# A four-layer graph network on one core: layer 1's small feature maps stand at two places per step, and its first two products run in halves by turns

## The chip, the core and the metric

The kernel runs on one core of a Trainium2 chip. The metric is device time in microseconds of one launch; the median of several runs is given. In the profile PE is the matrix engine (TensorE), PEld its weight loads, DVE the vector engine, ACT the scalar engine, POOL GpSimd, and SP the engine whose queue issues most of the DMAs.

## The reference, cut to what matters

Eight graphs `x` of 2048 nodes with 64 features share one adjacency matrix. Four layers follow one another, each of them residual behind a layer norm and a ReLU. The change is in layer 1, which repeats one update three times, and touches layer 2:

```python
# adj: 2048 x 2048, symmetric pattern, every row divided by its number of ones
h = maximum(layernorm(x), 0)                       # layer 1
v = h;  v[:, 0] = intervention_value
for _ in range(3):
    effects = einsum('nm,bmd->bnd', adj, v)
    t = relu(einsum('bnk,dk->bnd', concatenate([v, effects], -1), W1) + b1)
    v = einsum('bnk,dk->bnd', t, W2) + b2
x = x + v
h = maximum(layernorm(x), 0)                       # layer 2
agg = einsum('ij,bjf->bif', adj, h)
...
x = x + (einsum('bnf,of->bno', agg_nl, w_out) + b_out)
```

Layer 0 is a Chebyshev graph convolution with node-wise weights, and layer 3 an attention that comes down to the mean over the nodes for this input.

## The kernel before

**Tiling.** Graphs are worked on in pairs (`p` = 0 to 3), so that 2 x 64 features fill 128 partitions. The 2048 nodes are 16 chunks of 128 (index `m`) and 4 blocks of 512 (index `nb`). `BT` holds the pattern of the adjacency matrix as ones and zeros for the whole kernel; the division by the row's count is done on the result, with a row `crow` that is loaded anew for each block.

**A product.** `product(hl, nb, ...)` multiplies an operand by block `nb` of `BT`: for each of the 16 chunks two matmuls of 128x128 by 128x512 (L257), one with the high part `H` of the operand and one with the low rest `L`, 32 in all, into one PSUM bank of the tag "mm" (two banks). `fill` maps a chunk number to a function that is called behind that chunk, so that other work is written between the matmuls. `scaled` (L247, DVE) then multiplies the sum by `crow`. The operand `hl` is a list of four pairs (H, L), one for each block of 512 nodes; chunk `m` reads pair `m // 4`. `halves` makes a pair: a cast on ACT (L237) and a subtraction on DVE (L239).

**Layer 1.** The kernel folds W2 into the matrices of the next step, so that each of the three steps (`s`) of a pair has four products and two kinds of small maps, both made of 64x64 tiles because the two graphs of a pair are kept apart:

- `map_two(nb)` (L939, "ph" in the profile): the map of the previous features of blocks `nb` and `nb + 1`, four programmed matmuls of 512 columns, into two banks of the tag "big"; four copies on ACT (L945) put the result back in place. Before the change it is called at chunk 10 of blocks 0 and 2.
- `back_to_nodes` (L692, "bn"): the map of one block of new features back into node order, 16 programmed matmuls of 64 columns. `finish(nb)` calls it, and then for steps 0 and 1 adds a row (L924, DVE) and makes the pair of halves for the next step; in the last step it adds the map to `acc` (L920), which is x loaded from DRAM, and calls `keep`, which starts the next layer's norm, adds the bias on POOL (L731) and stores x (L732). `finish` of blocks 0 and 1 is called behind the products of blocks 1 and 2, that of block 2 at chunk 8 of block 3 (in the last step behind block 3), that of block 3 at the end of the step.

Between product and map stand the scaling, an addition of the mapped old features (L955, DVE) and the ReLU (L956, ACT). In steps 0 and 1 each block is also followed by two calls of `test`, a comparison on DVE (L885) of a part of the adjacency matrix with its transpose; three buffers of `st` and `mt` are loaded ahead on SP's queue.

In the last step of a pair `prepare_next` makes the operand of the next item block by block: it loads `h` from DRAM, and for layer 1 it writes the intervention row into block 0 (L720, ACT, behind the latest ReLU), transposes the block (L269), and maps it with another `back_to_nodes` ("bn_u") into halves.

**Order of the work.** The layer norm is a generator with three stages; `go_on` advances all pending ones by a stage. A planner sets the order on each engine when the kernel is built: it follows the program's order, but takes a later instruction where it expects an earlier one not to be ready, and `issue_after` pins an instruction behind another one of its engine. Tiles of one tag share a fixed number of buffers, and a tile that takes a buffer waits for the release of its last user. The last `finish(3)` of layer 1 is put off (`put_off`) and called at chunk 9 of the second block of layer 2.

Of the kernel before, what the change touches and what calls it, by code (L numbers as in the profile page):

```python
# [42 lines left out]
def uniform_path(  # L43
# [31 lines left out]
    P = 128  # L75
# [25 lines left out]
    def bank(tag, name):  # L101
        return psums[-1].tile([P, 512], F32, tag=tag, name=name)
# [69 lines left out]

    pending = []
    powers, firsts, variances, scales = [], [], [], []
    squares, lows, stored = [], [], []
    ahead = []
# [35 lines left out]
    def go_on():  # L214

        with tc.issue_after(ahead.pop().ins) if ahead else nullcontext():
            for e in list(pending):
                next(e[0])
                e[1] -= 1
                if e[1] == 0:  # L220
                    pending.remove(e)
        ahead.clear()

    def all_done():
        while pending:
# [18 lines left out]
    def scaled(ps, out, crow):  # L244

        crow, to = (a.rearrange("p (t q) -> p t q", t=4) for a in (crow, out))
        ahead.append(nc.vector.tensor_tensor(  # L247
            to, ps.rearrange("p (q t) -> p t q", t=4), crow, op=ALU.mult
        ))
        return out  # L250

    def product(hl, nb, name, out, crow, fill={}, tag="mm"):

        ps = bank(tag, f"bv_{name}")
        for m in range(NCH):
            for i in range(2):
                nc.tensor.matmul(  # L257
                    ps, hl[m // 4][i][:, m % 4, :], BT[:, m, nb * 512:(nb + 1) * 512],
                    start=(m == 0 and i == 0), stop=(m == NCH - 1 and i == 1),
                )  # L260
            if m in fill:
                fill[m]()
        return scaled(ps, out, crow)

    def transposed(src, name):

# [5 lines left out]
    def to_feat(h, out, name):  # L272
        pt = transposed(lambda t: h[:, t, :], name)
        nc.scalar.copy(out, pt.rearrange("p t n -> p (t n)"))
        return out
# [403 lines left out]

    two = (slice(0, C), slice(C, P))  # L680

    def back_to_nodes(fT, wmat, name):

        ps = psums[-1].tile([P, 2, 512], F32, tag="big", name=f"bn_{name}")
        for t in range(4):
            for hf in range(2):
                for bb in range(2):  # L690
                    at = t * P + hf * C
                    nc.tensor.matmul(  # L692
                        ps[two[hf], bb, t * C:(t + 1) * C],
                        fT[two[bb], at:at + C], wmat[two[bb], two[bb]], start=True, stop=True,
                    )
        return ps[:, :, :4 * C].rearrange("p b (t c) -> p t b c", c=C)

    def back_whole(fT, wmat, name):

# [7 lines left out]
    ops = {}  # L707
    relus = []

    def prepare_next(n, q):  # L710
        if n >= len(items):
            return
        layer, p = items[n]
        nm = f"{layer}_{p}_{q}"
        hl, gT = ops.setdefault(n, ([], []))
        h = load_h(p, q, nm, lastp[0] if n else l0q)
        if layer == 1:
            if q == 0:
                with tc.issue_after(relus[-1].ins) if relus else nullcontext():
                    nc.scalar.copy(h[0:1, 0, :], ivt)  # L720
            gT.append(to_feat(h, feat(0, f"gT_{nm}"), nm))
            h = (back_to_nodes if n else back_whole)(gT[q], w1e, f"u_{nm}")
        hl.append(halves(h, nm))

    def rows4(r):
        return r.rearrange("p (b c) -> p b c", b=2)[:, None].to_broadcast([P, 4, 2, C])

    def keep(p, nb, acc, name, more):

# [44 lines left out]
    for p in range(NP):  # L774
# [21 lines left out]
        def between(nb, t):  # L796

            if 4 * p + nb + 1 == 4 * NP:
                prepare_next(0, t)
            elif nb == 2 and t == 1:  # L800
                halve_next(0)
            elif nb == 3:
                halve_next(t + 1)
                if t == 0:
                    load_next(3)
# [94 lines left out]
        nc.tensor.matmul(pf[:1, :1], tot, ones[:, :1], start=True, stop=True)  # L900
        nc.vector.tensor_scalar(flag, pf[:1, :1], 0.0, None, op0=ALU.is_gt)

    put_off = []

    def layer1(n, p):
        hl, gT = ops[n]
        steps = 3  # L910
        for s in range(steps):
            last = s == steps - 1
            g_new, hl_new = [], []

            def finish(nb):
                nm = f"1_{p}_{s}_{nb}"
                if last:
                    acc = load_x(1, p, nb)
                    pn = back_to_nodes(g_new[nb], w2T, nm)
                    nc.vector.tensor_tensor(nodes(acc), pn, nodes(acc), op=ALU.add)  # L920
                    keep(p, nb, acc, f"2_{p}_{nb}", rows4(rbo))
                else:
                    pn = back_to_nodes(g_new[nb], w1e2, nm)
                    nc.vector.tensor_tensor(pn, pn, rows4(r1e), op=ALU.add)  # L924
                    hl_new.append(halves(pn, nm))

            def mid():
                if last:
                    prepare_next(n + 1, 2)
                else:  # L930
                    finish(2)

            def map_two(nb):

                ph = psums[-1].tile([P, 2, 512], F32, tag="big", name=f"ph_1_{p}_{s}_{nb}")
                w = w1v2 if s else w1vT
                for i in range(2):
                    for bb in range(2):
                        nc.tensor.matmul(  # L939
                            ph[two[bb ^ i], bb, :], w[two[bb], two[bb]], gT[nb + i][two[bb], :],  # L940
                            start=True, stop=True,
                        )
                for i in range(2):
                    for bb in range(2):
                        nc.scalar.copy(gT[nb + i][two[bb], :], ph[two[bb ^ i], bb, :])  # L945

            for nb in range(NB):
                nm = f"1_{p}_{s}_{nb}"
                crow = load_crow(nb, nm)
                g = feat((s + 1) % 2, f"g_{nm}")  # L950
                fill = {8: mid} if nb == 3 else {}
                if nb % 2 == 0:
                    fill[10] = lambda: map_two(nb)
                product(hl, nb, nm, g, crow, fill=fill)
                gadd = nc.vector.tensor_tensor(g, g, gT[nb], op=ALU.add)  # L955
                relus.append(nc.scalar.activation(g, g, AF.Relu, bias=b1s if s else b1c))  # L956
                g_new.append(g)
                go_on()
                if nb in (1, 2):
                    finish(nb - 1)  # L960
                    if last:
                        prepare_next(n + 1, nb - 1)
                if s < 2:
                    k = 2 * (8 * p + 4 * s + nb)
                    with tc.issue_after(gadd.ins):
                        test(k)
                        test(k + 1)
            if last:
                finish(2)
                prepare_next(n + 1, 3)  # L970
            if last and n == NP - 1:

                put_off.append(lambda: finish(3))
            else:
                finish(3)
            gT, hl = g_new, hl_new

# [9 lines left out]
    def finish2(g):  # L989
        p, nb = divmod(g, NB)  # L990
        nm = f"acc_2_{p}_{nb}"
        acc = term(1, nm) if p % 2 else feat(1, nm)
        acc = acc.rearrange("p (j f) -> p j f", j=4)
        accs.append(acc)
        fill_x(acc, 2, p, nb)
        pn = back_to_nodes(es[g], wos, f"2_{p}_{nb}")
        nc.vector.tensor_tensor(nodes(acc), pn, nodes(acc), op=ALU.add)
        norm_relu(acc, f"3_{p}_{nb}", lambda h: zs.update({g: h}))

# [47 lines left out]
    def layer2(n, p):  # L1047
        hl, _ = ops[n]

        def behind(g):  # L1050
            go_on()
            if g > 0:
                finish2(g - 1)
            if g % NB > 1:
                prepare_next(n + 1, g % NB - 2)

        for nb in range(NB):
            g = NB * p + nb
            nm = f"2_{p}_{nb}"
            crow = load_crow(nb, nm)  # L1060
            fill = {5: lambda: behind(g)}
            if g > 0:
                fill[12] = go_on
            if nb == 3:
                fill[8] = lambda: prepare_next(n + 1, 2)
            if g == 1:
                fill[9] = lambda: put_off.pop()()
            if g > 1:
                fill[15] = lambda: sums(g - 2)
            e = lastp[0].tile([P, 512], F32, tag="st", name=f"e_{nm}", bufs=3)  # L1070
            es.append(product(hl, nb, nm, e, crow, fill=fill))
            if g == 0:
                go_on()
        prepare_next(n + 1, 3)
        if p == NP - 1:
            go_on()
            finish2(g)
            sums(g - 1)
            all_done()
            sums(g)  # L1080
# [600 lines left out]
```

## Time and profile before

| what | value |
|---|---|
| runs | 1218.68, 1221.76, 1225.72 us (median 1221.76) |
| the profiled execution, its own time | 1220.42 us |
| its span, first to last instruction | 1218.7 us |
| mean granted clock of TensorE | 0.996 |
| layer 1, first to last big matmul | about 625.7 to 1059.6 us of the span |
| big matmuls "bv<-BT" of layers 1 and 2 (L257, H and L) | 2048, starts 0.2267 us apart when undisturbed |
| node maps with `g` (L692) | 1536 instructions, mean 224 ns |
| feature maps (L939, from `g` and `gT`) | 192 instructions, mean 615 ns |

In the profile one programmed fp32 matmul shows as two instructions, so one `back_to_nodes` is 32 of them and one `map_two` 8. Durations of matmuls overlap, since they are pipelined; distances between starts say what one costs. A row of the chain of waits has the start, the time that the piece took on the chain, the engine, the tile, the line and the number of instructions. A row of the timeline has start, duration, engine, line, operation, the tile written and those read, and the shape.

### The profile page before, as it was taken

How to read it: one execution, taken by the hardware profiler on the slowest of the kernel's cores; microseconds unless marked ns; L12 is line 12 of the kernel's file. 1: busy time of each engine (PE TensorE's matmuls, PEld its weight loads, DVE VectorE, ACT ScalarE, POOL GpSimd, SP SyncE). 2: the span in 40 equal slices, each digit the busy share in tenths (PEclk: the TensorE clock that was granted, in tenths of full speed). 3: DMA queues.
4: the chain of work that ended last, by engine and by line, in shares of the span. 5: the costliest groups of instructions: out<-in, count | busy, mean ns of one | idle time of the engine just before them, and what ended most of it. 6: DMA issues, size and time to landing. Idle time of an engine off the chain costs nothing.

```text
span 1218.7 us, 19540 instructions
## 1 busy us (share of the span) xinstructions
PE 1196.7 (98%) x7730; PEld 812.6 (67%) x7730; DVE 745.2 (61%) x1944; ACT 237.8 (20%) x377; POOL 229.4 (19%) x244
## 2 busy tenths in 40 slices
PE   9999999999999999999999999999999999999996
PEld 7765555555675557655567777777777777777774
DVE  5457888777757775477755535535543645576664
ACT  6610001000010000000022233223323323211100
POOL 5610222211121111011110013003100400241211
PEclk9999999999999999999999999999999999999998
DMA  9981333333332233122237526543653553443321
GB/s 357 356 200 51 93 109 113 82 82 84 91 104 65 65 91 87 54 66 65 61 79 177 126 87 161 128 98 113 163 128 82 150 143 95 128 153 118 118 67 45
DMA packets 99848, 141.24 MB, mean 116 GB/s; under 512 B 43772, under 2 KB 56572, under 8 KB 97700
## 3 DMA queue, kind: packets, MB, share of 16 engines
q1 hardware_dynamic: 81188, 79.16, 24.5%
q0 software_dynamic: 12256, 49.73, 13.9%
q10 hardware_dynamic: 6304, 11.01, 2.9%
q8 instruction: 63, 1.03, 0.3%
q14 instruction: 37, 0.30, 0.1%
HBM read 95.03 MB, written 35.66 MB: 107 GB/s over the span
## 4 chain that ended last, share of the span: by engine, by line
PE 89%; DVE 4%; DMA 3%; issue 1%; POOL 1%; ACT 1%; POOLq 0%; ACTq 0%; DVEq 0%; SPq 0%
PE bv L257 39%; PE y L750 26%; PE bn L692 3%; PE bv_1b L257 2%; PE bv_2b L257 2%; PE bv_3b L257 2%; PE ph L939 2%; PE bv_0b L257 2%; DMA x<-in_x_dram 1%; PE bv_0a L257 1%; PE bv_3a L257 1%; PE pt L269 1%; PE bv_2a L257 1%; PE bv_1a L257 1%; DVE acc L759 1%
## 5 line engine op out<-in xcount | busy, mean ns | idle before, releaser
L257 PE MATMUL bv<-BT,H 128*128 128x512 f32 x1024 | 411.1, 401 | 0.0
L257 PE MATMUL bv<-BT,L 128*128 128x512 f32 x1024 | 401.3, 392 | 0.0
L257 PEld LDWEIGHTS bv<-BT,H 128*128 128x128 f32 x1024 | 192.2, 188 | 62.9 <-issue 22.0
L257 PEld LDWEIGHTS bv<-BT,L 128*128 128x128 f32 x1024 | 192.4, 188 | 37.5
L759 DVE SCALAR_TENSOR_TENSOR acc<-y,emb,acc 128x128 f32<-128x128 f32 x512 | 176.1, 344 | 65.8 <-PE y L750 65.8
L759 DVE SCALAR_TENSOR_TENSOR odd<-y,emb,odd 128x128 f32<-128x128 f32 x448 | 153.2, 342 | 0.0
L750 PE MATMUL y<-wt,t0T 64*128 64x512 f32 x512 | 143.7, 607 | 2.4 <-DVE odd L759 1.7
L200 POOL TENSOR_TENSOR rstd<-var,mhalf 128x8 f32<-128x8 f32 x64 | 105.7, 1654 | 185.9 <-DVE var L197 184.5
L247 DVE TENSOR_TENSOR g<-bv,crow 128x512 f32<-128x512 f32 x48 | 33.2, 691 | 168.5 <-PE bv L257 168.5
L192 ACT ACTIVATE sq<-z 128x512 f32<-128x512 f32 x64 | 40.4, 632 | 396.8 <-DVE z L187 366.5
L750 PEld LDWEIGHTS y<-wt,t0T 64*128 64x128 f32 x512 | 45.8, 185 | 63.3 <-issue 57.1
L731 POOL TENSOR_TENSOR acc<-acc,b2r 128x512 f32<-128x512 f32 x16 | 22.2, 1389 | 317.2 <-DVE z L187 317.2
L731 POOL TENSOR_TENSOR acc<-acc,wl 128x512 f32<-128x512 f32 x16 | 20.5, 1279 | 288.0 <-DVE z L187 288.0
L750 PE MATMUL y<-wt,t1T 64*128 64x512 f32 x256 | 66.8, 589 | 0.0
L203 DVE SCALAR_TENSOR_TENSOR z<-z,rstd 128x512 f32<-128x512 f32 x64 | 44.7, 703 | 28.3 <-POOL rstd L200 28.2
L195 DVE TENSOR_REDUCE var<-sq 128x8 f32<-128x512 f32 x64 | 43.5, 680 | 13.4 <-ACT sq L192 13.4
L885 DVE SCALAR_TENSOR_TENSOR junk<-mt,cols,st 128x512 uint8<-128x512 bf16 x64 | 47.7, 745 | 3.4 <-DMA mt<-MD 3.0
L945 ACT COPY g<-ph 64x512 f32<-64x512 f32 x64 | 37.2, 581 | 48.5 <-PE ph L939 47.7
L750 PEld LDWEIGHTS y<-wt,t1T 64*128 64x128 f32 x256 | 27.1, 187 | 27.8 <-issue 27.8
L956 ACT ACTIVATE g<-g,b1s 128x512 f32<-128x512 f32 x32 | 23.1, 723 | 99.1 <-DVE g L955 98.9
L730 POOL DMA_DIRECT2D hs<-z x32 | 18.7, 585 | 125.8 <-DVE z L203 89.3
L187 DVE TENSOR_TENSOR z<-acc,mean 128x512 f32<-128x512 f32 x56 | 38.3, 691 | 6.1 <-DMA hs<-z 4.7
(225 smaller groups left out, 1657.0 us busy)
## 6 DMA issues: line engine op xcount, KB each, us to landing
BT<-in_adj_dram POOLq DMA_DIRECT2D x16, 1024.0 KB, 10.0
crow<-crowD SPq DMA_DIRECT2D x64, 256.0 KB, 3.4
st<-in_adj_dram SPq DMA_DIRECT2D x64, 256.0 KB, 3.9
hs<-z POOLq DMA_DIRECT2D x40, 256.0 KB, 3.1
xs<-acc POOLq DMA_DIRECT2D x32, 256.0 KB, 2.4
MD<-BT POOLq DMA_DIRECT2D x16, 512.0 KB, 5.6
acc<-xs SPq DMA_DIRECT2D x32, 256.0 KB, 3.4
hb<-hs SPq DMA_DIRECT2D x28, 256.0 KB, 3.6
```

What stands on the lines that cost most here:

```text
L187: firsts.append(nc.vector.tensor_tensor(split(z), nodes(xt), each(mean)[:, :, :, None].to_broadcast([P, 4, 2, C]), op=ALU.subtract))
L192: squares.append(nc.scalar.activation(sq, z, AF.Square))
L195: nc.vector.tensor_reduce(var, groups(sq), axis=AX.X, op=ALU.add)
L200: powers.append(nc.gpsimd.tensor_tensor(rstd, var, mhalf, op=ALU.pow))
L203: scales.append(nc.vector.scalar_tensor_tensor(groups(h), g, 0.0, rstd[:, :, None].to_broadcast([P, 8, C]), op0=ALU.max, op1=ALU.mult))
L257: nc.tensor.matmul(ps, hl[m // 4][i][:, m % 4, :], BT[:, m, nb * 512:(nb + 1) * 512], start=(m == 0 and i == 0), stop=(m == NCH - 1 and i ...
L692: nc.tensor.matmul(ps[two[hf], bb, t * C:(t + 1) * C], fT[two[bb], at:at + C], wmat[two[bb], two[bb]], start=True, stop=True,)
L731: nc.gpsimd.tensor_tensor(nodes(acc), nodes(acc), more, op=ALU.add)
L750: nc.tensor.matmul(y[:, bb, :], terms[k][hs_, ts], wt[hs_, k, dg * 512:(dg + 1) * 512], start=(k == 0), stop=(k == K - 1),)
L759: last = nc.vector.scalar_tensor_tensor(xj, yd, ec, old, op0=ALU.mult, op1=ALU.add)
L885: nc.vector.scalar_tensor_tensor(junk, mt, cols[:, i, :], st, op0=ALU.mult, op1=ALU.not_equal, accum_out=bad[:, i, q:q + 1],)
L945: nc.scalar.copy(gT[nb + i][two[bb], :], ph[two[bb ^ i], bb, :])
```

## The change

The arithmetic stays the same. The order in layer 1 and the shapes of two helpers change:

- `back_two` replaces `back_to_nodes` and maps one or two blocks into one PSUM tile of two banks; for two blocks the row is added in one DVE instruction of 1024 columns, and the halves are made for each block.
- `product` is split into `chunks` (some of the chunks) and the scaling. In each step the order is: first half of block 0; the maps of blocks 2 and 3 carried over from the step before (`carry`); `map_two(0)`; first half of block 1; second half of block 0; second half of block 1; block 2; `map_two(2)` and the maps of blocks 0 and 1; block 3. The maps of blocks 2 and 3 are then carried into the next step.
- `map_two` writes two single banks of the tag "tr" instead of one tile of the tag "big".
- In the last step the second block's `keep` is put into a list `later`, from which `go_on` takes one.
- `prepare_next` becomes `begin_next` (load, intervention row, transposes; for layer 2 the halves) and `halve_two` (the maps of two blocks and their halves). At a change of pair, blocks 0 and 1 of the next pair are begun at chunk 4 of block 3 and mapped at chunk 9, block 2 is begun at chunk 12, block 3 at chunk 4 of the next step's first half, and blocks 2 and 3 are mapped behind the carried maps.
- The carried maps of the very last step, now two blocks, are called at chunk 9 of the second block of layer 2.

```diff
@@ go_on @@
         ahead.clear()
+        if later:
+            later.pop(0)()
@@ product @@
         ps = bank(tag, f"bv_{name}")
-        for m in range(NCH):
+        chunks(ps, hl, nb, range(NCH), fill)
+        return scaled(ps, out, crow)
+
+    def chunks(ps, hl, nb, ms, fill={}):
+        for m in ms:
             for i in range(2):
                 nc.tensor.matmul(
...
@@ back_to_nodes @@
-    def back_to_nodes(fT, wmat, name):
+    def back_two(fTs, wmat, name):
         ps = psums[-1].tile([P, 2, 512], F32, tag="big", name=f"bn_{name}")
...
+        for i, fT in enumerate(fTs):
+            for t in range(4):
+                for hf in range(2):
+                    for bb in range(2):
+                        at = t * P + hf * C
+                        nc.tensor.matmul(
+                            ps[two[hf], bb, (4 * i + t) * C:(4 * i + t + 1) * C],
+                            fT[two[bb], at:at + C], wmat[two[bb], two[bb]],
+                            start=True, stop=True,
+                        )
+        return ps.rearrange("p b (t c) -> p t b c", c=C)
@@ prepare_next @@
-    def prepare_next(n, q):
+    def begin_next(n, q):
...
+        if layer == 2:
+            hl.append(halves(h, nm))
+            return
+        if q == 0:
+            with tc.issue_after(relus[-1].ins) if relus else nullcontext():
+                nc.scalar.copy(h[0:1, 0, :], ivt)
+        gT.append(to_feat(h, feat(0, f"gT_{nm}"), nm))
...
+    def halve_two(n, q):
+        if n < NP:
+            hl, gT = ops[n]
+            ps = back_two(gT[q:q + 2], w1e, f"u_{n}_{q}")
+            for i in range(2):
+                hl.append(halves(ps[:, 4 * i:4 * i + 4], f"u_{n}_{q + i}"))
@@ layer1 @@
+    carry = []
+
+    def step1(n, p, st, hl, gT):
...
+        def map_two(nb):
+            ph = [bank("tr", f"ph_{nm}_{nb}_{bb}") for bb in range(2)]
...
+        def finish_two(nb):
+            ps = back_two(g_new[nb:nb + 2], w2T if last else w1e2, f"{nm}_{nb}")
+            if not last:
+                nc.vector.tensor_tensor(ps, ps, rows4(r1e, 8), op=ALU.add)
+            for i in range(2):
+                pn = ps[:, 4 * i:4 * i + 4]
+                if last:
+                    acc = load_x(1, p, nb + i)
+                    nc.vector.tensor_tensor(nodes(acc), pn, nodes(acc), op=ALU.add)
+                    keep_it = lambda i=i, acc=acc: keep(
+                        p, nb + i, acc, f"2_{p}_{nb + i}", rows4(rbo)
+                    )
+                    later.append(keep_it) if i else keep_it()
+                else:
+                    hl_new.append(halves(pn, f"{nm}_{nb + i}"))
...
+        def add(nb):
+            g = g_new[nb]
+            gadd = nc.vector.tensor_tensor(g, g, gT[nb], op=ALU.add)
+            relus.append(nc.scalar.activation(g, g, AF.Relu, bias=b1s if st else b1c))
+            if not last:
+                k = 2 * (8 * p + 4 * st + nb)
+                with tc.issue_after(gadd.ins):
+                    test(k)
+                    test(k + 1)
+
+        halves_of = range(NCH // 2), range(NCH // 2, NCH)
+        ps0 = sums_of(0)
+        other = n > 0 and st == 0
+        chunks(ps0, hl, 0, halves_of[0], {4: lambda: begin_next(n, 3)} if other else {})
+        if carry:
+            carry.pop()()
+        if other:
+            halve_two(n, 2)
+        map_two(0)
+        ps1 = sums_of(1)
+        chunks(ps1, hl, 1, halves_of[0])
+        chunks(ps0, hl, 0, halves_of[1])
+        scale(ps0, 0)
+        add(0)
+        go_on()
+        chunks(ps1, hl, 1, halves_of[1])
+        scale(ps1, 1)
+        add(1)
+        go_on()
+        ps2 = sums_of(2)
+        chunks(ps2, hl, 2, range(NCH))
+        scale(ps2, 2)
+        map_two(2)
+        finish_two(0)
+        add(2)
+        go_on()
+        fill = {}
+        if last:
+            fill = {
+                4: lambda: (begin_next(n + 1, 0), begin_next(n + 1, 1)),
+                9: lambda: halve_two(n + 1, 0), 12: lambda: begin_next(n + 1, 2),
+            }
+        ps3 = sums_of(3)
+        chunks(ps3, hl, 3, range(NCH), fill)
+        scale(ps3, 3)
+        add(3)
+        go_on()
+        carry.append(lambda: finish_two(2))
+        return hl_new, g_new
...
@@ layer2 @@
             if g == 1:
-                fill[9] = lambda: put_off.pop()()
+                fill[9] = lambda: carry.pop()()
```

`sums_of(nb)` loads `crow` and takes an "mm" bank; `scale` is `scaled` into a new feature tile. `first_operand`, called in layer 0, begins and maps the first pair block by block as before.

## Prediction

> **What bounds the kernel now.** I read the page first: span, busy row, clock row.
>
> ```profile
> PE 1196.7 (98%) x7730; PEld 812.6 (67%) x7730; DVE 745.2 (61%) x1944; ACT 237.8 (20%) x377; POOL 229.4 (19%) x244
> ...
> PEclk9999999999999999999999999999999999999998
> ```
>
> TensorE is busy in every slice at full clock, so time is gained only by shortening its stream. The chain of waits, in order of time, shows what that stream is in layer 1. This is one whole step (pair 0, step 1), from a first big matmul after `map_two(0)` to the next such point:
>
> ```profile
> 666.86 9.76 PE bv L257 x42
> 676.62 0.62 PE bn L692 x32
> 677.25 5.21 PE bv L257 x22
> 682.46 1.02 PE ph L939 x8
> 683.48 2.51 PE bv L257 x10
> 685.99 0.62 PE bn L692 x32
> 686.62 4.30 PE bv L257 x18
> 690.92 0.62 PE bn L692 x32
> 691.55 5.89 PE bv L257 x25
> 697.44 0.62 PE bn L692 x32
> 698.07 2.72 PE bv L257 x11
> 700.79 1.02 PE ph L939 x8
> ```
>
> The 128 big matmuls (bv) of a step are cut at six places by 64x64 work: four node maps (bn, `back_to_nodes`) and two feature maps (ph, `map_two`). The chain never leaves TensorE here: the step, 34.95 us, is a sum of its instructions. The stage table agrees: in this window PE is busy all 34.95 us, DVE 16.41, ACT 9.66, POOL 0. What one place costs is seen in TensorE's timeline:
>
> ```profile
> 641.29 0.39 PE L257 MATMUL bv<-BT,L 128*128 128x512 f32 x1
> 641.60 0.69 PE L692 MATMUL bn<-wl,g 64*64 64x64 f32 x32
> 642.23 0.50 PE L257 MATMUL bv<-BT,H 128*128 128x512 f32 x1
> 642.57 0.39 PE L257 MATMUL bv<-BT,L 128*128 128x512 f32 x1
> 642.80 0.40 PE L257 MATMUL bv<-BT,H 128*128 128x512 f32 x1
> ```
>
> Starts (first column) are what to read, since durations overlap. Undisturbed, bv starts every 0.2267 us. Here the map starts 0.31 after the last bv (0.085 late), takes 0.63, and the second bv after it comes 0.34 after the first (0.11 late), the next ones 0.01 late. Over the whole step: 34.95 - 128 x 0.2267 (29.02) - 4 x 0.625 - 2 x 1.02 = 1.39, or **0.23 us per place** beyond the map itself. Last, two maps that happen to stand side by side (first transition between pairs):
>
> ```profile
> 736.77 0.69 PE L692 MATMUL bn_u<-w1e,gT 64*64 64x64 f32 x32 [0.15 <-ACT gT L274]
> 737.29 0.65 PE L692 MATMUL bn<-wl,g 64*64 64x64 f32 x32
> 737.87 0.50 PE L257 MATMUL bv<-BT,H 128*128 128x512 f32 x1
> ```
>
> Together 1.10 us, not 2 x 0.625 = 1.25: a lone map also contains about 0.15 us in which nothing overlaps its last instructions. The other two transitions show 1.09 for the same pair. (The bracket is a wait ahead of the pair and not in the 1.10.)
>
> **The change, part by part.** The arithmetic and the instructions of TensorE stay; the map order changes. A regular step has two places instead of six: A, after half of block 0 (carried maps of blocks 2 and 3 of the step before, then `map_two(0)`), and B, after block 2 (`map_two(2)`, then maps of blocks 0 and 1). Layer 1 has 12 steps. Before: 12 x 6 = 72 groups, 72 places. After: 12 A, 12 B, and one in layer 2: 25. So 47 joins: 24 of bn to bn (12 at B, 11 at A, one in layer 2), 23 of bn to ph (12 at B, 11 at A, since the first A has no carry).
>
> *bn to bn:* 0.23 + 0.15 = 0.38 by the rows above, x 24 = 9.1 us. A rule of the Trainium skill speaks against this ("TensorE: Matmul & The Clock Gate", section "Wait — 56ns, not 53.3ns?"): start to start never drops under about 25 ns however small the matmul. The row has 32 instructions in 0.52 us, 16 ns each. By the rule a pair would need 1.6 us, joining would save only the 0.23, and this term would be 5.5 us. The row is of this very instruction, so I take 9.1.
>
> *bn to ph:* no row has these two side by side. The 0.23 goes with the place: 5.3 us for 23. Whether the 0.15 goes too is open, from 0 (ph loads its weights only when the maps have ended) to 0.15 each (3.5 us). For the upper end speaks "TensorEngine Tiling (Array Packing)", section "Key Properties": a change of tiling mode drains the engine, a change of tile does not, and both are 64*64 in the rows. It would give 8.8 in all, the lower end 5.3. A ph instruction holds the array longer than a bn one (1.02 us for 8), so I take the middle, 7.1.
>
> *Transitions between pairs (three).* In TensorE's timeline, from ph to ph, the step with the change of pair takes 40.55, 40.21, 40.21 us, so 5.60, 5.26, 5.26 over a regular one: 16.1. In the new order it adds to a regular step: four transposes (`begin_next`), each 0.35 plus the 0.11 late bv after it (entering a 128*128 transpose shows no lateness): 1.84. `halve_two(n+1, 0)`, a place of two maps: 1.10 + 0.23 = 1.33. `halve_two(n, 2)` joins A: 2 x 0.52 = 1.04. Sum 4.2. For waits I add 0.5: the first transpose waits for the copy of `ivt` into `hb` (ACT L720), ordered behind the last ReLU, and that ReLU now stands behind the acc add and norm of block 0 on DVE. Before, the waits here were 0.6 once and 0.15 twice. So 3 x 4.7 = 14.1, a gain of 2.0. Bounds: -2 (the `ivt` copy and split places cost 1.3 more each) to +5 (no wait, transposes joined).
>
> *Moved at no cost, and the cover.* Interleaving halves of blocks 0 and 1: the bv run of 42 above crosses from one block and bank to the next at the same pace, so the turns cost nothing; block 2 needs block 0's bank, which `scale` frees 0.8 us after its end, under the 3.63 us of block 1's second half. The DVE adds of r1e go from two of 512 (2 x 0.69) to one of 1024 per place: between 0.69 and 1.39, beside PE's bv, on a DVE that is busy under half of the step. The ph tiles move to the "tr" banks, still one bank per row half. `crow` of block 1 is asked of SP 3.6 us sooner; `load_x` for two blocks stands together, and the second waits for POOL's add and `xs` store to free a buffer (two buffers; before, the second load likewise left only after such a store, at 719.76). SP behind it holds `crow` and test loads; DVE behind it holds the halves of the next operand. It happens at three transitions. From the end of the carried maps PE has 1.04 (`halve_two`) + 4.7 us of other work before it needs those halves; DVE needs two acc adds (2 x 0.69), the first operations of one norm (0.69 + 0.17 + 0.69) and one L (0.69), 3.6. The 2.2 us between them cover a late load; if it came 5 us late, each transition would cost some 3. In layer 2 one place of two maps replaces one map; the norm of its second block is put by `later` into the next `go_on` and is first needed by pair 3's products, some 90 us on.
>
> *The wait that is added.* Block 0's second half needs the operand halves 2 and 3 that A makes: PE waits, with everything behind it. The window is ph 0.86 plus late starts 0.25 plus 16 bv (3.63): about 4.7 us. The chain as it now stands takes 2.1 us (add at 698.13, cast, L239 ending 700.18, from a map end near 698.05); with the wider add an estimated 2.8. Slack 1.9. The carry itself needs block 3's ReLU: in the trace 2.2 us after its product (660.0 to 662.2), and 16 bv give 3.6. So no stall is in the sum. Without that cover, each 0.1 us of stall costs 1.1 us in all.
>
> **Sum:** 9.1 + 7.1 + 2.0 = 18.2 us. The profiled execution took 1220.42 (span 1218.7); 1220.4 - 18.2 = 1202.2. The median of the runs shown is 1.3 higher, 1221.76, giving 1203.6; I say 1203.5. What limits then is still TensorE's stream, with bv at 0.2267.
>
> **Rivals.**
> - *Late operands in part.* ACT may run its four ph copies (2.37 us together) before the two casts at A. Then cast and L end 4.7 us after the maps, slack zero, and a pair of tests (0.83 each) ahead on DVE makes PE stall 0.3 to 1 us a step, 3 to 11 us in all: 1207 to 1215. For: the copies are ready first. Against: the adds and casts stand earlier in the program.
> - *Places do not stay together.* The PE order in the trace is not the written one: `finish(3)` stands 11 bv into the next step, when its ReLU is ready. If the carried maps are judged unready they split off. With half of the joins lost (24 x 0.35 = 8.4 us) and a stall of 0.5 us in 11 steps, 3 to 4 us would be left: about 1218. Against: 16 bv is more than those 11. This is also the case of a change that does not do what it says.
> - *Slower: test loads on DVE's path.* Blocks 0 and 1 now end 3.6 us apart, so four tests compete for three st/mt buffers, whose loads take 3.9 us to land. A test that waits holds the DVE; if this reached A, the add of the carry would come late each step. It decides from 1.9 us of lateness on; cancelling 18 us needs 1.9 + 1.6 = 3.5 us in each of 11 steps, and 4.5 us give 1229 or more. For: tests are issued on DVE before the carry. Against: the waits view has 3.0 us for tests in all of layer 1, and the last tests before A follow their loads by over 5 us.
> - *More than summed.* No drain between any neighbours, no waits in the transitions: 9.1 + 8.8 + 5 = 22.9, about 1199, or lower.
>
> **How the numbers follow.** Main case 0.66 (1200 to 1208), more than summed 0.07 (1196 to 1200), partly late 0.16 (1207 to 1215.5), split or cancelled 0.06, slower 0.05. A difference under 0.5%, 6.1 us, is what a measurement of this kernel can hardly tell from none. Faster by more: 0.66 + 0.07 + 0.16 = 0.89. The range 1197 to 1214 leaves out the last two and the tails of others.
>
> **What would show it.** Right: per regular step two non-bv places, step length near 33.5; bn L692 and ph L939 neighbours without bv; after B and A one late start of 0.11 each. PE busy total down by about as much as the span. Wrong: PE idle before a bv with DVE L239 or the ACT cast of H as its releaser (late operands); more than two places per step (split); joined places longer than 2 x 0.52 + 0.9 plus drain, which puts the joins at 0.23 each and the time near 1209.

## The result, and the profile after

| | kernel before | changed kernel | ratio, 95% interval |
|---|---|---|---|
| first chip | 1220.54 us | 1205.75 us (1204.86 to 1207.68) | 0.9874 [0.984, 0.9908] |
| another chip | 1221.17 us | 1203.06 us (1201.77 to 1204.11) | 0.9852 [0.9835, 0.9869] |

The change takes 15 to 18 us off; 1203.5 was predicted, so the time was met. But two errors of the prediction cancel, and that is luck: layer 1 gained more than its sum, and layer 2, which the sum held at nothing, lost over 6 us.

The profiled execution took 1206.39 us. Its span, busy row and clock row:

```profile
span 1204.5 us, 19496 instructions
...
PE 1178.4 (98%) x7730; PEld 816.1 (68%) x7730; DVE 746.7 (62%) x1928; ACT 238.9 (20%) x377; POOL 231.7 (19%) x244
...
PEclk9999999999999999999999999999999999999998
```

TensorE's busy time fell by 18.3 us (from 1196.7), the span by only 14.2: TensorE has idle time now that it did not have. The page's slices are too coarse to show where. The chain of waits, in order of time, shows a regular step of layer 1 (the one from 664.26 to 697.64):

```profile
664.26 18.37 PE bv L263 x80
682.63 1.02 PE ph L944 x8
683.65 0.93 PE bn L699 x64
684.58 11.10 PE bv L263 x48
695.68 1.09 PE bn L699 x64
696.78 0.86 PE ph L944 x8
697.64 18.37 PE bv L263 x80
```

Six places have become two, B at 682.63 and A at 695.68. The second member of each place is shorter than the same map standing first: ph takes 0.86 instead of 1.02 and bn 0.93 instead of 1.09. What falls away is the end of the first map, in which nothing overlapped. TensorE's timeline at A has this in starts (first column):

```profile
661.92 0.39 PE L263 MATMUL bv<-BT,L 128*128 128x512 f32 x1
662.24 1.16 PE L699 MATMUL bn<-wl,g 64*64 64x64 f32 x64
663.22 1.04 PE L944 MATMUL ph<-g,wl 64*64 64x512 f32 x8
664.19 0.50 PE L263 MATMUL bv<-BT,H 128*128 128x512 f32 x1
664.52 0.39 PE L263 MATMUL bv<-BT,L 128*128 128x512 f32 x1
```

The place is entered once, 0.32 after the last bv, and left once, with the second bv 0.33 after the first. From ph to ph (663.22 to 696.60) the step takes 33.38 us instead of 34.95. The stage table (stretch, its length, then the busy time of PE, PEld, DVE, ACT and POOL, clock, DMA share, GB/s) shows TensorE busy all through it:

```profile
663.22:696.60 33.38, 33.38 (x286) 26.34 (x281) 16.39 (x30) 9.79 (x16) 0.00 (x0) 1.00 0.57 125
```

To see where the rest went I split TensorE's timeline at a landmark: the single small matmul "pf" that sums up the tests behind the last product of layer 1 (at 1060.24 us before, 1039.38 after).

| us | before | changed | difference |
|---|---|---|---|
| layer 1: its first big matmul to pf | 434.59 | 413.41 | -21.2 |
| layer 2: pf to the last node map that reads `e` | 139.58 | 145.87 | +6.3 |

In both kernels 1536 big matmuls stand ahead of pf, so the landmark cuts the stream at the same point. The two differences make 14.9 us; the other 0.7 of the span's 14.2 lies in the layers around.

Layer 2 is where the time was given back. In the waits of TensorE between 1030 and 1190 us, the kernel before has no row; the changed one has

```profile
PE bn L699 <- DVE e L249: 4.1, 3, 2.4
```

(us in total, times, longest). The longest stands at the entry to layer 2. First the map in the kernel before, which waits for nothing, then the changed kernel:

```profile
1070.56 0.69 PE L692 MATMUL bn<-wl,e 64*64 64x64 f32 x32
...
1049.39 0.39 PE L263 MATMUL bv<-BT,L 128*128 128x512 f32 x1
1052.13 0.69 PE L699 MATMUL bn<-wl,e 64*64 64x64 f32 x32 [2.35 <-DVE e L249]
1052.76 0.50 PE L263 MATMUL bv<-BT,H 128*128 128x512 f32 x1
...
1053.39 0.63 PE L263 MATMUL bv<-BT,H 128*128 128x512 f32 x1
1053.82 0.63 PE L263 MATMUL bv<-BT,L 128*128 128x512 f32 x1
```

The map waits 2.35 us for `e`, the first scaled product of layer 2. After it the big matmuls start 0.43 us apart instead of 0.2267. The stage table says why (the number ahead of the DMA share is the granted clock):

```profile
1049.60:1053.24 3.64, 1.29 (x35) 1.00 (x35) 1.64 (x3) 0.00 (x0) 1.75 (x2) 1.00 0.74 252
1053.24:1056.65 3.41, 3.41 (x28) 2.26 (x30) 2.55 (x5) 0.63 (x1) 0.00 (x0) 0.50 0.39 145
1056.65:1060.00 3.35, 3.35 (x67) 2.87 (x60) 2.65 (x7) 0.00 (x0) 1.66 (x1) 1.00 0.43 157
```

The clock is halved for 3.41 us, which costs 1.7 us. So the 6.3 us can be taken apart: 4.1 of waits, 1.7 of slow clock, and 0.46 for the second map of the put-off place (64 instructions take 1.09 us at full clock, 32 take 0.63) make 6.2.

Why `e` was late is read on DVE. The product had ended near 1046.8, and DVE stood idle twice before it got to the scaling:

```profile
1048.22 0.69 DVE L241 TENSOR_TENSOR L<-hb,H 128x512 fp32r<-128x512 f32 x1 [2.60 <-ACT H L239]
1048.83 0.16 DVE L197 TENSOR_SCALAR var<-var 128x8 f32<-128x8 f32 x1
1050.79 0.69 DVE L203 SCALAR_TENSOR_TENSOR z<-z,rstd 128x512 f32<-128x512 f32 x1 [1.79 <-POOL rstd L200]
1051.40 0.68 DVE L249 TENSOR_TENSOR e<-bv,crow 128x512 f32<-128x512 f32 x1
```

In these rows DVE starts nothing behind an instruction that waits. Ahead of the scaling stands the low half of the *next* pair's operand, which waits for its cast; the norm's variance behind it was ready long before, and its way over POOL (`rstd`) starts late. ACT's row names the origin:

```profile
1047.57 0.62 ACT L239 CAST H<-hb 128x512 fp32r<-128x512 f32 x1 [6.55 <-DMA hb<-hs]
1048.09 0.72 ACT L978 ACTIVATE g<-g,b1s 128x512 f32<-128x512 f32 x1
```

The cast waited 6.55 us for a load that SP issued when its buffer came free. The chain has that load as

```profile
1041.51 5.98 DMA hb<-hs
```

The buffer was freed late because the subtraction that read it ended at 1041.4, behind two norms on DVE: `finish_two` and the `go_on` behind it start them together. Two instructions of that stretch are also much longer than the 0.69 us that they take elsewhere, and both run beside POOL's addition of the bias:

```profile
1037.43 1.81 DVE L187 TENSOR_TENSOR z<-acc,mean 128x512 f32<-128x512 f32 x1
...
1039.76 1.68 DVE L241 TENSOR_TENSOR L<-hb,H 128x512 fp32r<-128x512 f32 x1
...
1037.41 1.28 POOL L753 TENSOR_TENSOR acc<-acc,wl 128x512 f32<-128x512 f32 x1 [70.47 <-DVE mean L186]
...
1039.57 1.31 POOL L753 TENSOR_TENSOR acc<-acc,wl 128x512 f32<-128x512 f32 x1
```

That is 2.1 us of delay ahead of the load; in the kernel before only one such collision stands here (a subtraction of 1.70 us at 1056.53). An estimate from these rows: without the two, and with all else unmoved, `e` would come 2.1 us sooner, and most of the 2.35 us of waiting would not be there. No run tested this.

The last ReLU of layer 1 stood behind the cast too. It did so in the kernel before as well (cast at 1061.87 after a wait of 2.63 us, ReLU at 1062.39), where no map waited for it.

### The profile page after: what moved, and what is told of

It reads as the page before. It is cut to its first block, busy times and chain, and to the rows that moved or that the text cites. A ratio compares the mean times of both kernels' runs of the same rounds, so it can differ in the third digit from the quotient of the medians.

```text
span 1204.5 us, 19496 instructions
## 1 busy us (share of the span) xinstructions
PE 1178.4 (98%) x7730; PEld 816.1 (68%) x7730; DVE 746.7 (62%) x1928; ACT 238.9 (20%) x377; POOL 231.7 (19%) x244
## 3 DMA queue, kind: packets, MB, share of 16 engines
q8 instruction: 63, 1.03, 0.4%
## 4 chain that ended last, share of the span: by engine, by line
PE 85%; DMA 5%; DVE 5%; POOL 2%; ACT 2%; issue 1%; POOLq 0%; ACTq 0%; DVEq 0%; SPq 0%
PE bv L263 36%; PE y L772 27%; DMA BT<-in_adj_dram 3%; PE bv_2b L263 2%; PE bv_1b L263 2%; PE bv_3b L263 2%; PE bn L699 2%; PE bv_0b L263 2%; PE ph L944 2%; PE pt L274 1%; PE bv_0a L263 1%; PE bv_3a L263 1%; PE bv_2a L263 1%; PE bv_1a L263 1%; POOL rstd L200 1%
## 5 line engine op out<-in xcount | busy, mean ns | idle before, releaser
L263 PE MATMUL bv<-BT,H 128*128 128x512 f32 x768 | 306.3, 399 | 0.0
L263 PE MATMUL bv<-BT,L 128*128 128x512 f32 x768 | 300.3, 391 | 0.0
L263 PEld LDWEIGHTS bv<-BT,H 128*128 128x128 f32 x768 | 144.4, 188 | 39.6 <-PE bn L699 6.5
L263 PEld LDWEIGHTS bv<-BT,L 128*128 128x128 f32 x768 | 144.7, 188 | 28.6
L263 PE MATMUL bv<-BT,H_u 128*128 128x512 f32 x256 | 100.9, 394 | 0.0
L263 PE MATMUL bv<-BT,L_u 128*128 128x512 f32 x256 | 99.8, 390 | 0.0
L263 PEld LDWEIGHTS bv<-BT,H_u 128*128 128x128 f32 x256 | 48.1, 188 | 13.2 <-issue 3.2
L263 PEld LDWEIGHTS bv<-BT,L_u 128*128 128x128 f32 x256 | 48.1, 188 | 9.7
```

The lines of the kernel that those rows point to most:

```text
L263: nc.tensor.matmul(ps, hl[m // 4][i][:, m % 4, :], BT[:, m, nb * 512:(nb + 1) * 512], start=(m == 0 and i == 0), stop=(m == NCH - 1 and i ...
```

## The experiments

The regular step and the two distances to and from pf (called layer 1 and layer 2 below) are used throughout. Median times are set against the kernel before on the same chip.

**1. The next pair's halves pinned behind the work that layer 2 needs first** (e1_pin), for the first pair of layer 2:

```diff
+                if g < NB:
+                    with tc.issue_after(relus[-1].ins), tc.issue_after(marks[-1].ins):
+                        begin_next(n + 1, g % NB - 2)
+                else:
                     begin_next(n + 1, g % NB - 2)
```

(`marks` collects the scalings of `scaled`.)

> The changed kernel with one edit: in layer 2's first pair the halves of the next pair's blocks 0 and 1 are pinned behind the last ReLU of layer 1 (ACT) and behind the newest scaled product (DVE). Theory (order): in the changed kernel ACT holds that ReLU and DVE holds the first scaling of layer 2 behind a cast whose load lands at 1047.57 of the span; this is what makes PE wait 2.4 us at 1049.7 and run at clock 0.67 to 0.71 until 1057.5. Then the first scaling comes near 1047, the wait and the slow stretch vanish, and the time falls by 4 to 6 us, to 1200 to 1202, with the clock back near 0.996. Rival (load): DVE is simply overfull after the step's two norms; the scaling then stays later than 1050, the wait stays over 1.5 us, and the time changes by under 1.5 us.

Measured: 1202.37 us, ratio 0.9856 [0.9839, 0.9873]. The first wait is gone: `e` is made at 1047.65 and the map starts on time at 1049.40. But the waits of layer 2 did not go away; they stand later and are nearly as long in sum (3.5 us instead of 4.1):

```profile
PE bn L700 <- DVE e L249: 3.5, 2, 2.2
```

The longer one is at 1069.84. DVE's timeline ahead of it:

```profile
1065.85 0.69 DVE L185 TENSOR_REDUCE mean<-acc 128x8 f32<-128x512 f32 x1
1067.68 0.69 DVE L203 SCALAR_TENSOR_TENSOR z<-z,rstd 128x512 f32<-128x512 f32 x1 [1.15 <-POOL rstd L200]
1068.29 0.16 DVE L186 TENSOR_SCALAR mean<-mean 128x8 f32<-128x8 f32 x1
1068.49 0.69 DVE L187 TENSOR_TENSOR z<-acc,mean 128x512 f32<-128x512 f32 x1
1069.10 0.68 DVE L249 TENSOR_TENSOR e<-bv,crow 128x512 f32<-128x512 f32 x1
```

Again a norm's stages, one of them waiting for POOL, ahead of a scaling whose product was done near 1064.3; TensorE's last big matmul before the wait starts at 1067.21. DVE is not full there, 4.67 of the 7.9 us from 1062.0 to 1069.9 are busy; it is held. So without the halves of the next operand in front there is no first wait, and norms that stand closely together are ahead of the later ones. Layer 2 takes 143.65 us, 2.2 less than in the changed kernel, where 4 to 6 us of the time were expected.

Repeated on another chip (e1_again):

> e1_pin once more, on the chip of these two, as their base: 1200.5 to 1203.5, PE waiting 2 to 4 us for scalings of layer 2.

Measured: 1204.2 us (1200.71 to 1205.79), 0.986 [0.9838, 0.9881], layer 2 143.98. In the length of layer 2 the pin is worth 1.5 to 2.2 us (against 145.87 and 145.47 in the two profiles of the changed kernel); in the medians of different chips it cannot be told from nothing, since all four intervals overlap.

**2. TensorE kept busy through the wait** (e5_warm): six small matmuls (twelve instructions in the profile) ahead of the waiting map.

```diff
             if g == 1:
+                keep_warm("tr", 6)
```

> The changed kernel with six idle-filling 128x128 fp32 matmuls put ahead of the map that PE waits for in layer 2 (they add no result). At the end of the kernel such matmuls take about 0.39 us each, so they fill about 2.3 of the 2.4 us. The wait for the scaling is not shortened. Theory (clock): the slow stretch after the wait is TensorE's clock, lowered because the engine stood idle; with the fill, bv after 1052 starts every 0.227 us, the clock there reads 1.00, and the time falls by about 2.4 us. Rival (contention): the stretch is slow because of what DVE, DMA or PSUM do then; the fill changes nothing of it and the time stays within 0.7 us.

Measured: 1203.11 us, 0.987 [0.9851, 0.9889]. TensorE's timeline:

```profile
1047.58 1.50 PE L108 MATMUL warm<-ones 128*128 128x128 f32 x12
1049.71 0.69 PE L699 MATMUL bn<-wl,e 64*64 64x64 f32 x32 [0.63 <-DVE e L249]
```

The fill takes 1.50 us, not the 2.3 expected. The idle stretch is down to 0.63 us, the big matmuls after it keep 0.2267 and the granted clock stays at 1.00. That fits a clock that answers idle time, though this run alone does not prove it: in e1_pin a wait of 2.24 us left the clock at 1.00 too. Layer 2 takes 144.92, only 0.95 us less (0.55 against the repeat). The fill stands where the wait was, so only the 1.7 us of slow clock could be won, and part of it is lost again: the next long wait, at 1069.71, is 1.81 us instead of 1.03.

**3. The 23 joins of node map and feature map undone** (e3_split): `map_two` stands two chunks away from its neighbour, everything else as in the changed kernel.

```diff
-        map_two(0)
         ps1 = sums_of(1)
-        chunks(ps1, hl, 1, halves_of[0])
+        chunks(ps1, hl, 1, range(2))
+        map_two(0)
+        chunks(ps1, hl, 1, range(2, 8))
...
-        chunks(ps2, hl, 2, range(NCH))
+        chunks(ps2, hl, 2, range(NCH), {13: lambda: map_two(2)})
         scale(ps2, 2)
-        map_two(2)
```

> The changed kernel with map_two parted from the node maps at both places by four bv: 23 joins of bn to ph are undone, nothing else. Theory (a join saves the switch and the drain): a regular step grows from 33.38 by 2 x 0.39 to 34.16, and the time grows by 23 x 0.39 = 9.0 us, to about 1214.7. Rival (the drain was never in a bn-ph join, only the switch): 33.84 a step, 23 x 0.23 = 5.3 us, about 1211. A map_two inside a block can't stall anything here, so waits should not change.

Measured: 1210.23 us, 0.9926 [0.9909, 0.9942]. The chain in this kernel:

```profile
662.80 1.12 PE bv L263 x4
663.92 1.02 PE ph L944 x8
664.94 16.55 PE bv L263 x72
681.48 1.02 PE ph L944 x8
682.50 1.12 PE bv L263 x4
683.63 1.09 PE bn L699 x64
684.72 11.11 PE bv L263 x48
695.82 1.09 PE bn L699 x64
```

A lone ph costs its 1.02 and makes the four bv beside it 0.21 longer than 4 x 0.2267: 1.23, against 0.86 next to a bn, so 0.37 per join. The whole step (663.85 to 697.97) says the same: 34.12, which is 0.74 more for two joins. That is the end of the first map as well as the edges of the place; the 0.23 of the edges alone is rejected. Layer 1 as a whole lost 7.5 us, 23 x 0.37 = 8.5 less 1.1: at a change of pair the four bv behind the carried maps cover the wait ahead of the first transpose (ten bv 2.40 instead of 2.76 us, three times). The time rose by less than that, because layer 2 took 143.33: its waits happened to be shorter (0.53, 1.81 and 0.72 us) and no slow clock followed. This helps to explain why the time lies nearer to the 1211 of the rival than to 1214.7.

**4. No turns between the first two products** (e4_noturns): blocks 0 and 1 as whole products, with the carried maps and `map_two(0)` still after half of block 0.

```diff
-        chunks(ps1, hl, 1, halves_of[0])
         chunks(ps0, hl, 0, halves_of[1])
...
-        chunks(ps1, hl, 1, halves_of[1])
+        chunks(ps1, hl, 1, range(NCH))
```

> The changed kernel without the turns: the second half of block 0 is written directly behind map_two(0), then all of block 1. Theory (the turns hide the operand chain): from the end of the carried maps the operand of chunk 8 takes 2.8 us in the trace (663.35 to 666.15), and PE has only ph 0.97, a late start and a few bv that the planner moves up, so it waits about 1.2 us at each of 8 regular A places and 2 or more at the three with a change of pair: 13 to 18 us more, 1219 to 1224. Rival (the planner finds the turns by itself): it moves block 1 up far enough, no wait, within 2 us of the changed kernel.

Measured: 1220.94 us, ratio 1.0011 [1.0, 1.0022]: all of the gain is lost. Waits of TensorE from 600 to 1200 us:

```profile
PE bv L263 <- DVE L_u L241: 6.8, 3, 2.5
PE bv L263 <- ACT H L239: 4.5, 8, 0.6
```

The first row is the three changes of pair (2.55, 2.39 and 1.86 us), the second the eight regular steps, 0.56 each and 0.90 in all with the bv behind it (step 34.28 us). Layer 1 takes 428.53, 15.1 more, so grouping without the turns keeps 6 of the 21 us there, and layer 2's loss (145.15, 5.6 more than before) takes these back. The turns are not an extra: they are the cover under which grouping pays.

**5. Where the two last norms of layer 1 start.** Four kernels start the norms of the last pair's blocks 2 and 3 later, through empty entries in `later`, and three of them have the pin of experiment 1 too.

```diff
+                    if n == NP - 1 and nb == 2 and i:
+                        later.extend([lambda: None] * 13 + [keep_it])
+                    else:
                         later.append(keep_it) if i else keep_it()
```

This is the last of the four (e10_pin_g8): block 3's norm moves to the third pair's first block of layer 2. e9_pin_g4 has 5 in place of 13. e7_pin_spread and e8_spread move the norms of both blocks (6 and 3 entries), with and without the pin.

> The kernel with the pin of e1_pin, and with the norms of the two last carried blocks started in layer 2's second pair (about chunk 12 of its blocks 0 and 2) instead of directly behind the carried maps. Theory (two causes): the order gave the first wait, the four norms close together on DVE and POOL give the later ones (3.5 us in e1_pin, both for the scaling of a layer 2 product). Then all waits of PE for a scaling fall under 1 us in sum, and the time is 3 to 4 us under e1_pin: 1198.5 to 1199.5. Rival (the next pair's halves and casts hold DVE, not the norms): waits stay over 2.5 us, and the time stays within 1 us of e1_pin.

> The changed kernel with the spread norms alone, without the pin. Theory (two causes): the first wait, about 2.4 us, stays, since what is put off comes behind it; the later waits (1.7 us in the changed kernel) go. Time 1202.5 to 1204 if the clock drops again after the first wait, 1.5 to 2.5 us lower if not. Rival (one cause, the overfull DVE): the first wait goes too, and the time is that of e7_pin_spread.

> e1_pin with the norm of the first carried block started directly behind the carried maps and that of the second one in layer 2's second pair, at chunk 5 of its block 0. Theory (DVE is full for some blocks of layer 2, and a norm must go where it is not): one extra norm in the first pair is what the kernel before had there too, without a wait, and block 0 of the second pair has neither outputs nor next operands to serve. Waits for scalings under 1.5 us in sum, 2 to 3 us less than e1_pin. Rival (any extra norm in these two pairs costs its wait, as in e7_pin_spread): waits of 2 us or more, the time within 1 us of e1_pin or above it.

> As e9_pin_g4, with the second norm started at chunk 5 of the third pair's block 0. Theory: as there, the time within 1 us of e9_pin_g4. Rival (every later block is as full as the second pair's blocks 2 and 3): a wait of 1 to 2.5 us appears in the third pair.

| kernel | median us | ratio, 95% interval | layer 2, us | waits of TensorE in layer 2, us |
|---|---|---|---|---|
| changed kernel, same chip as the next two | 1203.06 | 0.9852 [0.9835, 0.9869] | 145.47 | first 1.92, and later ones |
| e7_pin_spread | 1205.15 | 0.987 [0.9854, 0.9887] | 145.72 | 1.3 (1093.11), 2.41 (1115.22) |
| e8_spread | 1206.25 | 0.9883 [0.9864, 0.9902] | 147.82 | 2.05 (1050.28), 1.33, 2.40 |
| e1_again, same chip as the next two | 1204.2 | 0.986 [0.9838, 0.9881] | 143.98 | 2.2 (1069.47) |
| e9_pin_g4 | 1201.61 | 0.9842 [0.9829, 0.9856] | 143.67 | 1.9 (1077.30) |
| e10_pin_g8 | **1200.00** (1198.82 to 1200.2) | 0.9828 [0.9814, 0.9841] | 141.45 | 1.3 (1076.12) |

e7_pin_spread, e8_spread and e9_pin_g4 missed what was expected of their waits. The first pair of layer 2 ran without a wait in e7_pin_spread, but the norms came down on the second pair, and the sum was no better. e8_spread kept the first wait, as expected of the missing pin. e9_pin_g4 has 1.9 us of waiting where under 1.5 was expected, and a layer 2 within 0.3 us of e1_again, though its median is 2.6 us lower. Moving one norm only, and past both crowded pairs, does best. The one row of waits between 1030 and 1190 us that e10_pin_g8 has left:

```profile
PE bn L700 <- DVE e L249: 1.3, 1, 1.3
```

Against the same kernel without the moved norm (e1_again, same chip) the median is 4.2 us lower, but the four runs of e1_again spread from 1200.71 to 1205.79. In layer 2 of the two profiles it is 2.5 us: 0.9 less waiting, and the 1.7 us of slow clock that e1_again has and e10_pin_g8 has not. It is well under the kernel before. Under the changed kernel it is 4.0 to 4.4 us in layer 2; the intervals of the two ratios, from different chips, still touch.

**6. The carried maps not put off into layer 2** (e6_carry1): the last `carry` is called at the end of layer 1.

```diff
+            carry.pop()()
...
-            if g == 1:
-                fill[9] = lambda: carry.pop()()
```

> The changed kernel with its last carried maps called at the end of layer 1 instead of in layer 2; the planner then parts them, block 2 before the first product of layer 2 and block 3 eight bv into it. Theory (norms close together on DVE): four norms come even closer, PE waits longer for the first scalings of layer 2, and the time rises by 1 to 4 us over the changed kernel, of which 0.4 is the parted place. Rival (putting off is what brought the waits): no wait over 1 us at the start of layer 2, and 3 to 5 us less than the changed kernel.

Measured: 1206.72 us, 0.9895 [0.9873, 0.9918], so 3.7 us slower than the changed kernel on that chip, and layer 2 takes 148.62. The wait is another than expected. ACT:

```profile
1043.17 0.62 ACT L239 CAST H<-hb 128x512 fp32r<-128x512 f32 x1 [5.13 <-DMA hb<-hs]
1043.69 0.72 ACT L978 ACTIVATE g<-g,b1s 128x512 f32<-128x512 f32 x1
```

The map at the end of layer 1 waits 5.2 us for that ReLU, which stands behind a cast that waits for a load. In the changed kernel the same ReLU starts at 1048.09, behind the same cast, but its map comes at 1056.08 and waits for nothing. Putting the maps off did not cause the loss in layer 2; it hides a worse one.

**7. The changed kernel on another chip** (after_again), the second row of the first table:

> The changed kernel once more, on the chip of the other runs of this call, so that differences of a few us can be read. Both theories: 1204.5 to 1207. If the drop of the clock after the first wait is a matter of when the wait falls, its profile may show that stretch at full clock this time, with the wait itself still there.

The time is 1.4 us under the range expected. Its first wait was 1.92 us at 1050.02, again with a slow clock behind it.

## Why the prediction was right in its time and wrong in a step

The predicted gain was 18.2 us. Measured from the landmarks it is 21.2 in layer 1 less 6.3 in layer 2. The mechanism, fewer places in TensorE's stream, is what the gain comes from, as the step of 33.38 us and experiment 3 show; that the total came out within 0.4 to 2.3 us is owed to two errors of opposite sign.

| term | predicted | measured |
|---|---|---|
| bn to bn in layer 1 | 23 x 0.38 = 8.7 | 23 x 0.415 = 9.5 |
| bn to ph | 23 joins, 7.1 | 23 x 0.37 = 8.5 |
| changes of pair | 16.1 - 14.1 = 2.0 | 16.1 - 13.6 = 2.5 |
| layer 1's last group (one map) now in layer 2 | within the joins | about 0.6, paid back in layer 2 |
| **layer 1** | about 18 | **21.1** worked out, 21.2 measured |
| layer 2 | at nothing (one join saved) | **-6.3** |

- *bn to bn* stood: a regular step is 1.57 shorter for four joins; with 0.37 for the two ph joins by experiment 3, 0.83 is left for two bn joins, 0.415 each. This is a remainder, so the sum of 21.1 shows that the parts add up, and is no second measurement. The 25 ns from start to start, which the prediction weighed and set aside, do not hold in the place itself: 64 instructions on four 64x64 tiles take 0.93 to 1.09 us, about 16 ns each.
- *bn to ph* was mis-sized: 0.31 us per join was summed, 0.37 was measured. The prediction took half of the 0.15 us in which nothing overlaps the end of a map; all of it goes. This is the upper end, which it had drawn from the Trainium skill ("TensorEngine Tiling (Array Packing)", section "Key Properties"): a change of tiling mode drains, a change of tile does not. Experiment 3 agrees with it, at 0.37 us per place avoided.
- *Changes of pair* stood: 37.92 us three times, 4.54 over a regular step, where 4.7 was summed.
- *The wait that is added* stood: at A the maps end near 663.35, the low half of block 2's operand ends at 666.15, 2.8 us later as estimated, and TensorE reads it near 668.0. The slack is 1.9 us, and no step stalls. Block 3's low half ends only at 667.98, since ACT put two of its copies between the two casts; it is read near 669.7. Experiment 4 showed what it would cost without that cover: 15.1 us.
- *"In layer 2 one place of two maps replaces one map"*, at nothing, is the step that failed. The second map alone costs 0.46 us. The other 5.8 us are waits (4.1) and the slow clock behind the longest (1.7). The prediction asked when the norm of the second block is *needed*, some 90 us on, and found it covered; it did not ask what DVE and ACT would have in their queues while two norms start at once, next to the first scalings of layer 2. Experiment 1 shows that the first wait needs the halves of the next operand in front of the scaling, though not that this order is enough: the two DVE instructions lengthened beside POOL lie on the same chain. Experiment 5 shows that moving the norms moves the later waits, and that one placement takes most of them away; experiment 6, that putting off the maps was not the cause.
- *The rivals.* No operand at A came too late, no place was split, no test held A. "More than summed" was true of layer 1 and false of the time. The sum of "places do not stay together" leaves 4.3 us of gain, not 3 to 4; nothing hangs on it.

The same three parts give layer 2 in other runs (its length less the 139.58 of the kernel before): e1_pin 3.5 + 0 + 0.46 = 4.0 against 4.1, e1_again 2.25 + 1.7 + 0.46 = 4.4 against 4.4, e10_pin_g8 1.3 + 0 + 0.46 = 1.8 against 1.9. What stays open is how much of the first wait is owed to the order of the queues, how much to the two lengthened instructions, and why the clock falls after some waits only.

## What to carry to other kernels

When maps are grouped, their sources come due together as well: list what the grouped step starts on each in-order queue, and look for anything in front of the next critical instruction that waits for a load or for another engine, above all at a change of stage. A queue that is about 60% busy can still be late, because one waiting instruction at its head holds all that is ready behind it. Fix the order first, then see where the wait goes: it can come back one stage later, and only the distance between landmarks, not the wait that went, tells what was gained.

## What the runs showed of the hardware

- **A short idle time can halve the clock for 3.4 us.** After waits of TensorE of 1.8 to 2.4 us (in layer 2 of the changed kernel, its repeat, e4_noturns, e7_pin_spread, e8_spread, e9_pin_g4 and e1_again) the granted clock was 0.50 for 3.41 us, beginning 0.6 to 1.6 us after the end of the wait, with big matmuls 0.43 us apart. In e6_carry1, after 5.2 us, it was 0.50 for the 5.83 us behind the wait. Between 600 and 1190 us of the thirteen profiles the clock fell nowhere else. After others of the same length it stayed at 1.00 (2.24 in e1_pin, 1.81 in e5_warm and e3_split, 2.40 in e8_spread, and 2.55, 2.39 and 1.86 at the changes of pair in e4_noturns). The shortest wait with a fall behind it is 1.54 us (e7_pin_spread, at 46.27 us, in layer 0). The same wait of the same kernel did both, 2.24 in e1_pin and 2.25 in e1_again. The Trainium skill ("TensorE: Matmul & The Clock Gate", section "Part 1: The HAM clock gate") has a gate of half or full rate, decided over windows of about 3.4 us that run freely. The 3.41 us measured agree, and free windows would fit a cost that depends on where the wait falls; no run tested that. Its bound for harmful idle gaps (section "HAM oscillation", over about 3.4 us) does not hold here, by the waits just listed.
- **A place of 64x64 work between 128x128 work costs 0.37 to 0.42 us** beyond its instructions, for both kinds of map here: 0.23 at its two edges, the rest in the end of its last map, in which nothing overlaps.
- **One DVE addition of 1024 columns from PSUM** took 1.23 us. Two DVE instructions of 512 columns take 0.69 each, but 1.28 back to back, since they overlap a little: almost nothing is saved.
- **DVE instructions beside a POOL addition can be held.** Between 600 and 1200 us of the changed kernel six DVE instructions of at most 512 columns lasted 1.40 to 1.81 us; all six overlap a bias addition on POOL. Five of the six have 512 columns and read two operands from SBUF. Those that read one of the two from PSUM kept 0.68 to 0.69 beside the same additions (`L_u<-bn_u,H_u`, nine times).
